# Decay factors of a state space layer: from PSUM one pair ahead to SBUF five pairs ahead

## The chip, the cores and the metric

The kernel runs on one core of a Trainium2 chip. The metric is the device time of one launch in microseconds (us). A core has TensorE (matrix products; PE in the profile, with PEld for its weight loads), VectorE (DVE), ScalarE (ACT), GpSimd (POOL) and SyncE (SP), which issues the DMAs here. Each engine works through its own queue in order, and they wait for one another by semaphores. SBUF is the on-chip working memory; PSUM, of eight banks, takes the results of TensorE.

## The reference

Two residual layers on an image batch `x` of 4 x 384 x 64 x 64, all in float32. Layer 0 is a state space layer: group norm, layer norm, a projection to 2 x 768 channels, a causal convolution of width 4, SiLU, a projection to the step `dt` and to B and C (16 states each), the recurrence, a gate, and a projection back. Layer 1 is attention in 7 x 7 windows. The change is in the recurrence of layer 0:

```python
dt = jax.nn.softplus(jnp.einsum('blr,dr->bld', dt, dt_w) + dt_b)
A = -jnp.exp(A_log)
def step(h, inp):
    dt_t, B_t, C_t, x_t = inp
    dA = jnp.exp(dt_t[:, :, None] * A[None])
    dBx = (dt_t * x_t)[:, :, None] * B_t[:, None, :]
    h = dA * h + dBx
    y_t = jnp.einsum('bdn,bn->bd', h, C_t)
    return (h, y_t)
...
y = jnp.moveaxis(ys, 0, 1) + xc * D
y = y * _silu(z)
out = jnp.einsum('bld,cd->blc', y, out_proj_w)
```

It runs over 4,096 time steps for each of 4 images, 768 channels and 16 states.

## The kernel before

Channels lie on the 128 partitions (six tiles `d` of 128), time along the free dimension. A step `I` takes 256 time steps of one image, so there are 4 x 16 = 64 steps. A *group* is four of the sixteen states (`g`) of one channel tile: 64 x 6 x 4 = 1,536 groups. In each group ScalarE computes the decay factors exp(A dt) for four states, VectorE runs four scans, GpSimd and VectorE multiply the states by C, and TensorE sums them. Beside this, a plan of 48 slots per step carries the preparation of the next steps (norms, projections, convolution, softplus) in between; one slot runs after each half group.

GpSimd makes the driving term `db` = dt x B of a group, two groups ahead:

```python
def driven(I, d, g, h):
    ...   # at g == 0: dtx = dt * xc, 128 x 256, on GpSimd
    db = w2.tile([P, NG, T], F32, tag="db", ..., bufs=3)
    nc.gpsimd.tensor_tensor(
        db, h["dtx"].unsqueeze(1).broadcast_to([P, NG, T]), h["bc"][g][0], ALU.mult
    )
    return db
```

The group itself. `ps_a` (two banks) holds the decay factors `da`, a pair of states to a bank; `ps_h` (one bank) holds the states `hp` of the first pair; those of the second pair, `hs`, lie in SBUF:

```python
def scan(I, d, g, h, db, y, ahead):
    dt = h["dt"][d // 2][:, d % 2, :]
    ct = h["bc"][g][1]
    hp = ps_h.tile([P, 2, T], F32, tag="hp", name="hp")
    hv = w2.tile([P, 2, T], F32, tag="hv", name="hv")
    hs = w2.tile([P, 2, T], F32, tag="hs", name="hs", bufs=4)
    for half, to in ((0, hp), (1, hs)):
        da = ps_a.tile([P, 2, T], F32, tag="da", name="da")
        n = g * NG + 2 * half
        for k in range(2):
            act(da[:, k, :], dt, AF.Exp, scale=nega[:, d, n + k : n + k + 1])
        for k in range(2):
            nc.vector.tensor_tensor_scan(
                to[:, k, :], da[:, k, :], db[:, 2 * half + k, :],
                state[:, d, n + k : n + k + 1] if I % NCHUNK else 0.0,
                ALU.mult, ALU.add,
            )
            if half == 1 and k == 0:
                nc.vector.tensor_copy(state[:, d, n - 2 : n], hp[:, :, T - 1])
                nc.vector.tensor_tensor(hv, hp, ct[:, 0:2, :], ALU.mult)
        ahead()          # one slot of the preparation

    def with_c():        # called during the next group
        nc.gpsimd.tensor_copy(state[:, d, n : n + 2], hs[:, :, T - 1])
        nc.gpsimd.tensor_tensor(hs, hs, ct[:, 2:4, :], ALU.mult)

    def summed(t):       # TensorE: transposes of hv or hs, summed in y
        ...
```

Two more places matter. Softplus ends with three VectorE instructions in one slot, each with a PSUM input (`pb`). And the group norm of each image, and of layer 1, works on three numbers per partition in SBUF:

```python
def added():             # softplus
    pb, dt = t["pb"], t["dt"]
    nc.vector.scalar_tensor_tensor(pb, pb, -1.0, t["e"], ALU.add, ALU.subtract)
    nc.vector.tensor_tensor(pb, t["r"], pb, ALU.subtract)
    nc.vector.tensor_tensor(dt, dt, pb, ALU.add)

def deviation():         # group norm; dev, mv and gm lie in SBUF
    nc.vector.tensor_copy(gm[:, :, 0], t["psmc"][:, 0:NJ])
    nc.vector.tensor_tensor(dev, mv[:, :, 0:1], gm[:, :, 0:1], ALU.subtract)
    nc.vector.tensor_tensor(dev, dev, dev, ALU.mult)
    nc.vector.tensor_tensor(dev, dev, mv[:, :, 1:2], ALU.add)
```

PSUM in layer 0: two banks for `da`, one for `hp`, two for `y`, three for the preparation. The weights of the attention layer, `w_qkv` and `w_pj`, are loaded at the start of the kernel and stay in SBUF throughout.

Of the kernel before, what the change touches and what calls it, by code (L numbers as in the profile page):

```python
# [8 lines left out]
F32 = mybir.dt.float32  # L9
AF = mybir.ActivationFunctionType  # L10
ALU = mybir.AluOpType
PSUM = bass.MemoryType.PSUM
DRAM = bass.MemoryType.DRAM

P = 128
# [10 lines left out]
NX = DTR + 2 * NS  # L26
T = 256
NCHUNK = L // T
TX = 512
NXT = L // TX  # L30
GROUPS = 32
# [17 lines left out]
def two_layers(  # L49
# [45 lines left out]
    def act(o, i, func, **kw):  # L95
        ins = nc.scalar.activation(o, i, func, **kw)  # L96
        return in_order(ins) if func in tabled else ins
# [54 lines left out]
    def load(shape, src, name):  # L152
        t = const.tile(shape, F32, name=name)
        nc.sync.dma_start(t, src)
        return t
# [41 lines left out]
    for j in range(NJ):  # L197
        nc.vector.tensor_scalar(w_in[:, j, :], w_in[:, j, :], lnw[:, j : j + 1], None, ALU.mult)


    w_qkv = const.tile([P, NJ, 3 * C], F32, name="w_qkv")
    nc.sync.dma_start(w_qkv, qkv_wT.rearrange("(k p) m -> p k m", p=P))
    w_pj = load([P, NJ, C], proj_wT.rearrange("(k p) m -> p k m", p=P), "w_pj")
    with tc.tile_pool(name="ps_vb", bufs=1, space=PSUM) as fps:
        pb0 = fps.tile([P, 512], F32, name="pvb")
        for m in range(NJ):
            for j in range(NJ):
                nc.tensor.matmul(
                    pb0[:, m : m + 1], w_pj[:, j, m * P : (m + 1) * P], qkb[:, 2 * NJ + j : 2 * NJ + j + 1],
                    start=(j == 0), stop=(j == NJ - 1),  # L210
                )
        nc.vector.tensor_tensor(pjb, pjb, pb0[:, :NJ], ALU.add)

    state = const.tile([P, ND, NS], F32, name="state")
    xb = const.tile([P, ND, KC - 1 + T], F32, name="xb")

# [66 lines left out]
    def layer0(x1s, mvs):  # L283

        with ExitStack() as es:
            es.enter_context(tc.manual_schedule(engines=in_step))
            ps_a = es.enter_context(tc.tile_pool(name="ps_a", bufs=2, space=PSUM))
            ps_h = es.enter_context(tc.tile_pool(name="ps_h", bufs=1, space=PSUM))
            ps_y = es.enter_context(tc.tile_pool(name="ps_y", bufs=2, space=PSUM))
            ps = es.enter_context(tc.tile_pool(name="ps0", bufs=3, space=PSUM))  # L290
            bc = es.enter_context(tc.tile_pool(name="bc", bufs=4))
            w1 = es.enter_context(tc.tile_pool(name="w1", bufs=1))
            w2 = es.enter_context(tc.tile_pool(name="w2", bufs=2))
# [116 lines left out]
            def prepared(I, h, at):  # L410
# [82 lines left out]
                def softplus(q, first):  # L493

                    t = {}

                    def project():
                        t["pb"] = bank()
                        for k in range(2):
                            nc.tensor.matmul(  # L500
                                t["pb"][:, k, :],
                                w_dt[:, (2 * q + k) * P : (2 * q + k + 1) * P],
                                h["xd"][:DTR, :], start=True, stop=True,
                            )

                    def parts():
                        t["e"] = w2.tile([P, 2, T], F32, tag="sp_e", name=f"spe_{b}_{i}_{q}")
                        t["r"] = w2.tile([P, 2, T], F32, tag="sp_r", name=f"spr_{b}_{i}_{q}")
                        for k in range(2):
                            bias = dtb[:, 2 * q + k : 2 * q + k + 1]  # L510
                            act(t["e"][:, k, :], t["pb"][:, k, :], AF.Abs, bias=bias)
                            act(t["r"][:, k, :], t["pb"][:, k, :], AF.Relu, bias=bias)

                    def exped():
                        act(t["e"], t["e"], AF.Exp, scale=-1.0)
                        act(t["pb"], t["e"], AF.Identity, bias=1.0)

                    def logged():
                        t["dt"] = w2.tile([P, 2, T], F32, tag="dt", name=f"dt_{b}_{i}_{q}", bufs=4)
                        act(t["dt"], t["pb"], AF.Ln)  # L520

                    def added():
                        pb, dt = t["pb"], t["dt"]
                        nc.vector.scalar_tensor_tensor(
                            pb, pb, -1.0, t["e"], ALU.add, ALU.subtract
                        )
                        nc.vector.tensor_tensor(pb, t["r"], pb, ALU.subtract)
                        nc.vector.tensor_tensor(dt, dt, pb, ALU.add)
                        h["dt"].append(dt)

                    at(first, project)
                    at(first + 2, parts)
                    at(first + 3, exped)
                    at(first + 4, logged)
                    at(first + 5, added)

                for q in range(ND // 2):
                    softplus(q, 33 + 3 * q)
# [13 lines left out]
                )  # L552
                return db

            def scan(I, d, g, h, db, y, ahead):



                dt = h["dt"][d // 2][:, d % 2, :]
                ct = h["bc"][g][1]  # L560
                hp = ps_h.tile([P, 2, T], F32, tag="hp", name="hp")
                hv = w2.tile([P, 2, T], F32, tag="hv", name="hv")
                hs = w2.tile([P, 2, T], F32, tag="hs", name="hs", bufs=4)
                for half, to in ((0, hp), (1, hs)):
                    da = ps_a.tile([P, 2, T], F32, tag="da", name="da")
                    n = g * NG + 2 * half
                    for k in range(2):
                        act(da[:, k, :], dt, AF.Exp, scale=nega[:, d, n + k : n + k + 1])
                    for k in range(2):
                        nc.vector.tensor_tensor_scan(  # L570
                            to[:, k, :], da[:, k, :], db[:, 2 * half + k, :],
                            state[:, d, n + k : n + k + 1] if I % NCHUNK else 0.0,
                            ALU.mult, ALU.add,
                        )
                        if half == 1 and k == 0:
                            nc.vector.tensor_copy(state[:, d, n - 2 : n], hp[:, :, T - 1])
                            nc.vector.tensor_tensor(hv, hp, ct[:, 0:2, :], ALU.mult)  # L577
                    ahead()

                def with_c():  # L580
                    nc.gpsimd.tensor_copy(state[:, d, n : n + 2], hs[:, :, T - 1])  # L581
                    nc.gpsimd.tensor_tensor(hs, hs, ct[:, 2:4, :], ALU.mult)  # L582

                def summed(t):

                    for k in range(2):
                        first = g == 0 and t is hv and k == 0
                        last = g == NS // NG - 1 and t is hs and k == 1
                        for half in range(2):
                            nc.tensor.matmul(  # L590
                                y[:, half, :], t[:, k, half * P : (half + 1) * P], ident,
                                is_transpose=True, start=(first and half == 0),
                                stop=(last and half == 1), skip_group_check=True,
                            )

                return with_c, lambda: summed(hv), lambda: summed(hs)

            def turned(I, d, h, yt):

# [107 lines left out]
            run(-2)  # L707
            run(-1)
            work = [(I, d, g) for I in range(STEPS) for d in range(ND) for g in range(NS // NG)]
            AHEAD = 2  # L710
            dbs = [driven(*w, steps[w[0]]) for w in work[:AHEAD]]
            before = []
            for n, (I, d, g) in enumerate(work):
                slots = iter(range(2 * (n % (SLOTS // 2)), SLOTS))

                def ahead():
                    s = next(slots)
                    run(I, s, s + 1)

                if g == 0:  # L720
                    steps[I]["yt"][d] = ps_y.tile([P, 2, P], F32, tag="y", name="y")
                if before:
                    before[0][0]()
                if n + AHEAD < len(work):
                    nxt = work[n + AHEAD]
                    dbs.append(driven(*nxt, steps[nxt[0]]))
                if before:
                    before[0][1]()
                if len(before) > 1:
                    before.pop()[2]()  # L730
                before.insert(
                    0, scan(I, d, g, steps[I], dbs.pop(0), steps[I]["yt"][d], ahead)
                )
            before[0][0]()
            before[0][1]()
            before[1][2]()
            before[0][2]()
            run(STEPS)

    def layer1(x1s, mvs):  # L740
        scale = HD**-0.5
        with ExitStack() as es:
# [6 lines left out]

            bias = wt.tile([P, NH, NK], F32, name="bias")  # L750
            nc.sync.dma_start(bias.rearrange("p h k -> p (h k)"), bm)
            gms, vds = [], []
            for b in range(NB):
                gms.append(small.tile([P, NJ, 2], F32, tag="gm1", name=f"gm_b{b}", bufs=NB))
# [329 lines left out]
```

## Time and profile before

| | |
|---|---|
| time, median of three | 9,433.48 us (9,431.37 to 9,436.09) |
| span of the profiled execution | 9,436.4 us |
| busy share over the span | TensorE 83%, VectorE 79%, GpSimd 65%, ScalarE 61% |
| layer 0, first scan to last product of GpSimd | 111.8 to 6,797.7 us |
| VectorE / GpSimd busy from 6,900 us on (2,536 us) | 1,458 / 84 us |

The page gives, for every group of like instructions, the line, the engine, output<-inputs by the tile's name, partitions x elements, the count, then the busy time in us, the mean length of one in ns, and the idle time of the engine ahead of it with what ended it. Records of one engine overlap a little at their ends, so the distance from start to start in the timeline is somewhat less than an instruction's recorded length. [...] A view of the busy time by stretch tells the two layers apart; the shares of the whole span mix them. L96 is the helper that issues every activation.

### The profile page before, as it was taken

What the parts mean: (1) busy time and instruction counts of PE and PEld (TensorE: products, weight loads), DVE (VectorE), ACT (ScalarE), POOL (GpSimd) and SP (SyncE); (2) the same over time, 40 slices, a digit from 0 to 9 for tenths busy, and PEclk for the clock granted to TensorE, in tenths of its full rate; (3) what the DMA queues carried; (4) which work ended last, traced back from release to release, by engine and by line L of the source; (5) the groups of instructions that cost most, each with busy time, mean ns of one, the idle gap of its engine ahead of it and who ended that gap; (6) DMA issues with size and microseconds to landing.
All of it is one profiled execution on the core that took longest, in us unless ns stands there. A gap on an engine that the chain in (4) does not pass through costs nothing.

```text
span 9436.4 us, 139560 instructions
## 1 busy us (share of the span) xinstructions
PE 7804.9 (83%) x46266; PEld 5722.8 (61%) x46266; DVE 7485.8 (79%) x15348; ACT 5773.9 (61%) x13694; POOL 6104.2 (65%) x5271
## 2 busy tenths in 40 slices
PE   7877887788777877787788777877789999999999
PEld 5666666666666666666666666666545555555555
DVE  6888988898889888988898888888755555555555
ACT  5666666666766676666666766676444444444444
POOL 5888988898989898988889989998700000000000
PEclk8887888788878888888788888887699999999999
DMA  3111111111111111111111111111122222222222
GB/s 107 51 49 61 54 51 43 58 54 51 49 59 55 47 45 61 54 51 49 59 50 47 43 57 48 47 43 59 51 72 77 67 80 76 74 77 78 75 76 62
DMA packets 301912, 557.92 MB, mean 59 GB/s; under 512 B 61916, under 2 KB 185580, under 8 KB 301060
## 3 DMA queue, kind: packets, MB, share of 16 engines
q1 hardware_dynamic: 301188, 549.00, 18.4%
q8 instruction: 365, 5.98, 0.3%
q14 instruction: 359, 2.94, 0.1%
HBM read 446.33 MB, written 84.73 MB: 56 GB/s over the span
## 4 chain that ended last, share of the span: by engine, by line
PE 36%; DVE 28%; ACT 16%; POOL 10%; issue 9%; DMA 0%; SPq 0%; DVEq 0%; ACTq 0%; POOLq 0%
DVE hp L570 9%; DVE hs L570 8%; POOL db L550 5%; DVE hv L577 5%; PE mm_ps L628 5%; ACT da L96 4%; POOL hs L582 4%; PE y L590 3%; ACT sg L96 3%; PE mm_ps L393 3%; PE lg_ps L887 3%; PE mm_ps L969 3%; PE mm_ps L792 3%; PE mm_ps L855 3%; PE pt_ps L912 2%
## 5 line engine op out<-in xcount | busy, mean ns | idle before, releaser
L96 ACT ACTIVATE da<-dt,nega 128x256 f32<-128x256 f32 x6144 | 2922.8, 477 | 1416.8 <-DVE hs L570 972.3
L550 POOL TENSOR_TENSOR db<-dtx,B 128x1024 f32<-128x1024 f32 x1536 | 3620.9, 2357 | 30.1
L570 DVE TENSOR_TENSOR_SCAN hs<-da,state,db 128x256 f32<-128x256 f32 x2880 | 2118.6, 736 | 347.8 <-ACT da L96 347.8
L570 DVE TENSOR_TENSOR_SCAN hp<-da,state,db 128x256 f32<-128x256 f32 x2880 | 2153.8, 748 | 303.0 <-POOL state L581 192.9
L582 POOL TENSOR_TENSOR hs<-hs,C 128x512 f32<-128x512 f32 x1536 | 1952.2, 1271 | 123.2 <-POOL state L581 0.8
L590 PE MATMUL y<-ident,hv 128*128 128x128 f32 x6144 | 1192.0, 327 | 960.5 <-DVE hv L577 953.8
L590 PEld LDWEIGHTS y<-ident,hv 128*128 128x128 f32 x6144 | 850.5, 165 | 1409.5 <-DVE hv L577 1292.1
L96 ACT ACTIVATE sg<-sg,mx 128x308 f32<-128x308 f32 x1536 | 830.0, 541 | 890.1 <-DVE mx L893 889.8
L946 POOL COPY rb<-rsum 128x384 f32<-128x384 f32 x128 | 65.4, 511 | 2017.0 <-DVE rsum L944 1901.5
L590 PE MATMUL y<-ident,hs 128*128 128x128 f32 x6144 | 1156.4, 321 | 137.1 <-POOL hs L582 135.6
L393 PE MATMUL mm_ps<-xn,w_in 128*128 128x256 f32 x4608 | 1163.9, 404 | 2.0 <-DVE xn L369 2.0
L577 DVE TENSOR_TENSOR hv<-hp,C 128x512 f32<-128x512 f32 x1536 | 1044.3, 680 | 0.0
L590 PEld LDWEIGHTS y<-ident,hs 128*128 128x128 f32 x6144 | 901.8, 169 | 184.0 <-POOL hs L582 180.4
L393 PEld LDWEIGHTS mm_ps<-xn,w_in 128*128 128x128 f32 x4608 | 925.3, 207 | 133.3 <-issue 3.4
L893 DVE CUSTOM_DVE_ANT_0 sg<-lg_ps,bias 128x308 f32<-128x308 f32 x1536 | 650.4, 474 | 261.1 <-PE lg_ps L887 258.4
L400 PE MATMUL mm_ps<-xb,dcv 128*128 128x256 f32 x3072 | 716.9, 379 | 0.0
L581 POOL COPY state<-hs 128x2 f32<-128x2 f32 x1536 | 289.7, 189 | 523.6 <-DVE hs L570 461.9
L400 PEld LDWEIGHTS mm_ps<-xb,dcv 128*128 128x128 f32 x3072 | 567.6, 190 | 72.5
L500 PE MATMUL mm_ps<-xd,w_dt 24*128 24x256 f32 x768 | 335.4, 577 | 289.9 <-DVE yg L617 287.0
L628 PE MATMUL mm_ps<-yg,w_out 128*128 128x256 f32 x2304 | 520.9, 380 | 0.0
L917 DVE COPY ta<-pt_ps 110x512 f32<-110x512 f32 x768 | 495.4, 680 | 24.1 <-PE pt_ps L912 21.4
L927 ACT COPY tb<-pt_ps 88x512 f32<-88x512 f32 x384 | 223.1, 581 | 392.2 <-PE pt_ps L923 392.2
(139 smaller groups left out, 10832.0 us busy)
## 6 DMA issues: line engine op xcount, KB each, us to landing
B<-bcrows SPq DMA_DIRECT2D x256, 512.0 KB
C<-bcrows SPq DMA_DIRECT2D x256, 512.0 KB
vw<-vd SPq DMA_DIRECT2D x1792, 33.0 KB
xr<-x SPq DMA_DIRECT2D x28, 1056.0 KB
vd<-v SPq DMA_DIRECT2D x280, 96.0 KB
xi<-in_x_dram SPq DMA_DIRECT2D x64, 384.0 KB
x<-xo SPq DMA_DIRECT2D x64, 384.0 KB
o<-x SPq DMA_DIRECT2D x96, 256.0 KB
```

The lines of the kernel that those rows point to most:

```text
L96: ins = nc.scalar.activation(o, i, func, **kw)
L393: nc.tensor.matmul(pb[:, k, :], w_in[:, j, m * P : (m + 1) * P], xn[:, j, :], start=(j == 0), stop=(j == NJ - 1),)
L400: nc.tensor.matmul(pb[:, k, :], dcv[:, d, c, :], xb[:, d, c : c + T], start=(c == 0), stop=(c == KC - 1),)
L500: nc.tensor.matmul(t["pb"][:, k, :], w_dt[:, (2 * q + k) * P : (2 * q + k + 1) * P], h["xd"][:DTR, :], start=True, stop=True,)
L550: nc.gpsimd.tensor_tensor(db, h["dtx"].unsqueeze(1).broadcast_to([P, NG, T]), h["bc"][g][0], ALU.mult)
L570: nc.vector.tensor_tensor_scan(to[:, k, :], da[:, k, :], db[:, 2 * half + k, :], state[:, d, n + k : n + k + 1] if I % NCHUNK else 0.0, AL ...
L577: nc.vector.tensor_tensor(hv, hp, ct[:, 0:2, :], ALU.mult)
L582: nc.gpsimd.tensor_tensor(hs, hs, ct[:, 2:4, :], ALU.mult)
L590: nc.tensor.matmul(y[:, half, :], t[:, k, half * P : (half + 1) * P], ident, is_transpose=True, start=(first and half == 0), stop=(last an ...
L628: nc.tensor.matmul(h["po", first][:, m - first, :], w_out[:, d, m * P : (m + 1) * P], h["yg"][d], start=(d == 0), stop=(d == ND - 1),)
L893: nc.vector.tensor_tensor_reduce(sg[:, hh, :], lg[:, :NK], bias[:, 4 * m + hh, :], -1.0, BIG, ALU.add, ALU.min, mx[:, hh : hh + 1],)
L917: nc.vector.tensor_copy(t[: KN[0], :, :].rearrange("p a q -> p (a q)"), pt[: KN[0], :])
```

## The change

It gives the decay factors a longer lead and moves the recurrence out of PSUM:

- `da` lies in SBUF, in seven buffers of a pair each, and ScalarE writes it five pairs ahead of the scans (before: two PSUM banks, just ahead of them).
- All four scans of a group write one SBUF tile `hs`. The product with C of the first pair is done in place by VectorE, of the second pair in place by GpSimd, both during the next group.
- The last column of all four states is kept by one VectorE instruction (a maximum of the column with itself). GpSimd no longer copies states.
- The three banks set free go to the preparation: six in place of three. The three VectorE instructions of softplus are spread over three slots.
- To make room in SBUF, the attention weights, and the small product with `w_pj`, move to the start of layer 1.

It is meant to keep the scans from waiting for ScalarE, which leaves its exponentials once in a step for SiLU and two table loads.

```diff
+LEAD = 5
-    w_qkv = const.tile([P, NJ, 3 * C], F32, name="w_qkv")
-    ...                                   # moved to layer1, with w_pj and pvb
-            ps_a = es.enter_context(tc.tile_pool(name="ps_a", bufs=2, space=PSUM))
-            ps_h = es.enter_context(tc.tile_pool(name="ps_h", bufs=1, space=PSUM))
-            ps = es.enter_context(tc.tile_pool(name="ps0", bufs=3, space=PSUM))
+            ps = es.enter_context(tc.tile_pool(name="ps0", bufs=6, space=PSUM))
...
-                    at(first + 5, added)
+                    at(first + 5, lost)
+                    at(first + 6, linear)
+                    at(first + 7, added)
...
-            def scan(I, d, g, h, db, y, ahead):
-            ...
+            def decay(I, d, g, half, h):
+                da = w2.tile([P, 2, T], F32, tag="da", name="da", bufs=LEAD + 2)
+                dt = h["dt"][d // 2][:, d % 2, :]
+                n = g * NG + 2 * half
+                for k in range(2):
+                    act(da[:, k, :], dt, AF.Exp, scale=nega[:, d, n + k : n + k + 1])
+                return da
+
+            def scans(I, d, g, half, h, da, db, hs, between):
+                for k in range(2):
+                    j = 2 * half + k
+                    n = g * NG + j
+                    nc.vector.tensor_tensor_scan(
+                        hs[:, j, :], da[:, k, :], db[:, j, :],
+                        state[:, d, n : n + 1] if I % NCHUNK else 0.0,
+                        ALU.mult, ALU.add,
+                    )
+                    if k == 0:
+                        between()
+
+            def product(d, g, h, hs, y):
+                ct = h["bc"][g][1]
+                def kept_and_first():
+                    end = hs[:, :, T - 1]
+                    nc.vector.tensor_tensor(
+                        state[:, d, g * NG : (g + 1) * NG], end, end, ALU.max
+                    )
+                    nc.vector.tensor_tensor(hs[:, 0:2, :], hs[:, 0:2, :], ct[:, 0:2, :], ALU.mult)
+                def second():
+                    nc.gpsimd.tensor_tensor(hs[:, 2:4, :], hs[:, 2:4, :], ct[:, 2:4, :], ALU.mult)
+                ...
+                return kept_and_first, second, summed
...                                        # in the loop over groups:
+                hs = w2.tile([P, NG, T], F32, tag="hs", name=f"hs_{I}_{d}_{g}", bufs=4)
+                db = dbs.pop(0)
+                for half in range(2):
+                    if 2 * n + half + LEAD < len(halves):
+                        nxt = halves[2 * n + half + LEAD]
+                        das.append(decay(*nxt, steps[nxt[0]]))
+                    between = after[0][0] if half == 0 and after else lambda: None
+                    scans(I, d, g, half, steps[I], das.pop(0), db, hs, between)
+                    if half == 0:
+                        if after:
+                            after[0][1]()
+                        if n + AHEAD < len(work):
+                            nxt = work[n + AHEAD]
+                            dbs.append(driven(*nxt, steps[nxt[0]]))
+                        if len(after) > 1:
+                            after.pop()[2]()
+                    s = 2 * n + half
+                    run(I, s % SLOTS, s % SLOTS + 1)
+                after.insert(0, product(d, g, steps[I], hs, steps[I]["yt"][d]))
```

## The prediction

> **What bounds the kernel now.** I read the page's busy shares first, then the busy time by stretch, which tells the two layers apart: the state space layer runs from about 112 us to 6,800 us, the attention layer after it. The change alters the first alone. The columns are the stretch, its length, and the busy time and instructions of each engine.

> ```profile
> core 0: us, PE busy (x) PEld busy (x) DVE busy (x) ACT busy (x) POOL busy (x), PEclk, DMA share, GB/s
> ...
> 3000.00:5000.00 2000.00, 1590.26 (x7822) 1291.99 (x7822) 1784.23 (x3208) 1359.28 (x2979) 1791.68 (x1507) 0.82 0.16 52
> ```

> VectorE and GpSimd are both busy for 89% of these 2,000 us; TensorE for 80%, ScalarE for 68%. So two engines run side by side near their limits. The groups on the page say with what (count, busy us, mean ns of one, idle before):

> ```profile
> L550 POOL TENSOR_TENSOR db<-dtx,B 128x1024 f32<-128x1024 f32 x1536 | 3620.9, 2357 | 30.1
> L570 DVE TENSOR_TENSOR_SCAN hs<-da,state,db 128x256 f32<-128x256 f32 x2880 | 2118.6, 736 | 347.8 <-ACT da L96 347.8
> L570 DVE TENSOR_TENSOR_SCAN hp<-da,state,db 128x256 f32<-128x256 f32 x2880 | 2153.8, 748 | 303.0 <-POOL state L581 192.9
> L582 POOL TENSOR_TENSOR hs<-hs,C 128x512 f32<-128x512 f32 x1536 | 1952.2, 1271 | 123.2 <-POOL state L581 0.8
> ...
> L577 DVE TENSOR_TENSOR hv<-hp,C 128x512 f32<-128x512 f32 x1536 | 1044.3, 680 | 0.0
> ```

> [...]From the first scan (111.8 us) to the end of the last product on GpSimd (6,797.7 us) a group takes 6,686 / 1,536 = 4.35 us. The chain of waits for the stretch 3,000 to 5,000 us (458 groups) shows where VectorE idles:

> ```profile
> DVE hs L570 <- ACT da L96: 112.7, 74, 3.1
> DVE hp L570 <- POOL state L581: 61.3, 19, 3.6
> DVE hp L570 <- ACT da L96: 11.9, 18, 1.3
> ```

> Together 186 us, or 0.41 us a group. These are the waits that the change goes after: a longer lead of the exponentials, and no copy of the state on GpSimd.

> The line that decides is elsewhere. VectorE's tensor_tensor on `dev_a` has three elements a row and both inputs in SBUF. Here are VectorE and, below, GpSimd at the same time (start us, us, engine, line):

> ```profile
> 4799.84 0.47 DVE L264 TENSOR_TENSOR dev_a<-mv,gm_a 128x3 f32<-128x3 f32 x1
> 4800.34 0.16 DVE L265 TENSOR_TENSOR dev_a<-dev_a 128x3 f32<-128x3 f32 x1
> 4800.53 1.26 DVE L266 TENSOR_TENSOR dev_a<-dev_a,mv 128x3 f32<-128x3 f32 x1
> ```
> ```profile
> 4797.93 2.36 POOL L550 TENSOR_TENSOR db<-dtx,B 128x1024 f32<-128x1024 f32 x1
> 4800.22 0.20 POOL L581 COPY state<-hs 128x2 f32<-128x2 f32 x1
> 4800.50 1.28 POOL L582 TENSOR_TENSOR hs<-hs,C 128x512 f32<-128x512 f32 x1
> ```

> L264 ends at 4800.31, as GpSimd's L550 does (4800.29); L266 ends at 4801.79, as L582 does (4801.78). The same instruction in the attention layer, where GpSimd is idle:

> ```profile
> L266 DVE TENSOR_TENSOR dev_b<-dev_b,mv x4: 161/161/161, 6814.2 to 6832.5; 128x3 f32<-128x3 f32 x4
> ```

> 0.16 us against 1.26 us: a VectorE instruction with two SBUF inputs stands still until GpSimd's tensor_tensor is through. The reader should now look at the loop: scan (`da` in PSUM, `db` in SBUF), `hv` (`hp` in PSUM, C in SBUF), softplus, gate, residual, each has one input in PSUM. `hv` took 680 ns in every group (673 to 684), whatever GpSimd did.

> [...] a scan of 256 columns into SBUF starts 0.64 us after the one before it, a tensor_tensor of 512 columns 0.60 us. [...] here `da` (PSUM) takes 477 ns and `xn`, SBUF to SBUF with one pointer more, 585 ns. No trace here has `da` in SBUF.

> **The change, part by part**, per group:
> 1. *Exponentials in SBUF, five pairs ahead.* Four activations remain, at most 585 instead of 477 ns, so up to 0.4 us more on ScalarE, which has 4.35 x 0.32 = 1.4 us free. What it removes is up to 0.25 to 0.27 us of VectorE's idle time (112.7 + 11.9 us over 458 groups). What it adds: every scan now has both inputs, `da` and `db`, in SBUF.
> 2. *Scans to SBUF.* The two of a group that wrote PSUM start 0.72 us apart (two `hp` scans take 1.44 us), those that write SBUF 0.64: saves 2 x 0.08 = 0.16 us.
> 3. *The state copy* moves from GpSimd (0.19 us, with its start gap 0.27) to one VectorE tensor_tensor, and `hv` becomes a product in place, `hs` by C. Both have two SBUF inputs. Lengths 0.1 (my choice between the copy's 0.05 and the 0.19 of a dependent small tensor_tensor) and 0.60 us.
> 4. *Six banks for the preparation, softplus in three slots, the attention weights loaded later.* Same instructions. The weights are 128 x 4,608 x 4 bytes = 2.36 MB; at the 164 GB/s that the turn between the layers shows this is 14 us, once. I count 0 to 15 us.

> [...] VectorE: 4 scans x 0.64 + 0.60 + 0.1 = 3.26 us. GpSimd: L264 ended 0.02 us after L550 though it needs 0.16 alone, so GpSimd lets go about 0.14 us ahead of its record's end: 2.36 - 0.14 = 2.22 for `db`, 1.27 - 0.14 = 1.13 for the product, (0.73 - 0.14) / 4 = 0.15 for `dtx`; 3.50 us. VectorE's other instructions (softplus, gate, norm, statistics: the remaining rows of the groups by form in that stretch add up to some 265 us, 0.58 us a group) read PSUM or one SBUF input and can run beside GpSimd, but the queue is in order; I count half, 0.29. Sum 3.26 + 3.50 + 0.29 = 7.05, less 0.15 that I choose for the start of VectorE's instructions, done while they wait: **6.9 us a group**. Against 4.35 that is 2.55 x 1,536 = 3,917 us more: 9,433 + 3,917 = **13,350 us**. The 0.41 us of idle that the longer lead takes away doesn't help, since it stands beside a longer serial path.

> **Rivals.**
> - *It works as meant* (no contention). VectorE would need 4 x 0.64 + 0.60 + 0.1 + 0.58 = 3.84 us, GpSimd 2.29 + 1.23 + 0.2 = 3.72 us from start to start. With little idle left, some 3.95 us a group: 9,433 - 0.4 x 1,536 = about 8,800 us. Against it: the two waits on `dev_a`, and that the `hv` product has just the form of L266.
> - *Only the tensor_tensors contend, the scan doesn't.* No scan in this trace has two SBUF inputs, so it isn't excluded. GpSimd's 3.72 plus 0.60 plus 0.1 is 4.4 us at the least, and some VectorE time lost behind it: 4.4 to 4.9 us, 9,500 to 10,300 us.
> - *ScalarE or TensorE becomes the bound.* TensorE is busy 1,590 / 458 = 3.47 us a group, ScalarE 2.97 + 0.4. Both stay below 4.35, so neither alone makes it slower.

> **Range and chances.** A group time of 6.1 to 7.5 us covers what I chose: [...] how the two engines alternate. That is 9,433 + 1.75 x 1,536 = 12,100 to 9,433 + 3.15 x 1,536 = 14,300 us (rounded). The whole of it rests on the scan contending; I give the first rival 4 in 100 and the second about 10, of which some 4 end within 2%. So faster by over 2%: 0.04; within 2%: 0.04; slower by over 2%: 0.92.

> **What the profile after will show.** If right: scan records with a mean well over 1 us, a share of them near 0.65 and others about one GpSimd instruction longer; VectorE and GpSimd both busy nearly all of a layer that is 10 to 11 ms long[...]; records of `db` longer than 2.36 us where GpSimd waits in turn; no waits of scans for `da`; a TensorE clock no lower than now. The attention layer stays at 2.5 ms. Wrong: scans of 0.64 to 0.75 us each while `db` runs[...].

## The result and the profile after

The changed kernel takes **13,101 us** (median of four, 13,099.76 to 13,103.59) against 9,435 us before on the same chip: a ratio of 1.389, interval 1.386 to 1.391. The prediction was 13,350 us, in a range of 12,100 to 14,300.

The busy time by stretch, as it was shown for before (VectorE 1,784 us, GpSimd 1,792 us of 2,000 there):

```profile
3000.00:5000.00 2000.00, 1270.41 (x5056) 911.07 (x5056) 1989.63 (x2079) 854.23 (x1915) 1387.20 (x679) 0.72 0.11 35
```

VectorE is busy for 99.5% of it and runs a third fewer instructions (2,079 for 3,208). The groups on the page say which became longer:

```profile
L559 DVE TENSOR_TENSOR_SCAN hs<-da,state,db 128x256 f32<-128x256 f32 x5760 | 8091.8, 1448 | 0.0
L97 ACT ACTIVATE da<-dt,nega 128x256 f32<-128x256 f32 x6144 | 2784.5, 500 | 5882.7 <-DVE hs L559 5881.9
...
L580 POOL TENSOR_TENSOR hs<-hs,C 128x512 f32<-128x512 f32 x1536 | 2623.6, 1708 | 3120.1 <-DVE state L574 2589.3
L540 POOL TENSOR_TENSOR db<-dtx,B 128x1024 f32<-128x1024 f32 x1536 | 4173.3, 2717 | 30.1
```

A scan takes 1,448 ns on the mean, not 736 or 748. Its idle time is 0.0: no scan waits for a semaphore, and the exponentials wait 5,882 us for the scans. What the change went after is gone. In its place the scan itself is longer: it stands still while it counts as busy. GpSimd's instructions are longer too, 2,717 for 2,357 ns and 1,708 for 1,271: it waits in its turn.

One group in the timelines of VectorE and GpSimd (start us, us):

```profile
5022.45 0.13 DVE L574 TENSOR_TENSOR state<-hs 128x4 f32<-128x4 f32 x1
5022.61 0.69 DVE L577 TENSOR_TENSOR hs<-hs,C 128x512 f32<-128x512 f32 x1
5023.22 5.74 DVE L559 TENSOR_TENSOR_SCAN hs<-da,state,db 128x256 f32<-128x256 f32 x4
```
```profile
5022.72 1.71 POOL L580 TENSOR_TENSOR hs<-hs,C 128x512 f32<-128x512 f32 x1 [2.03 <-DVE state L574]
5024.39 2.73 POOL L540 TENSOR_TENSOR db<-dtx,B 128x1024 f32<-128x1024 f32 x1
```

They take turns. GpSimd's product (issued 5022.72) waits for VectorE's product (`hs` by C, to 5023.30) and then runs to 5024.43. The first scan, issued at 5023.22, waits for it. `db`, issued at 5024.39, waits for that scan, then holds the next one until 5027.12. Scans of 1.75 and 2.77 us are followed by two of 0.72, while GpSimd has nothing to do and waits for the next group's state. The least and the greatest length of all scans are near those of this group, and most scans have one of its three lengths: of 5,760, 2,645 take 0.7 to 0.8 us, 1,440 take 1.7 to 1.8 and 897 take 2.7 to 2.8.

```profile
L559 DVE TENSOR_TENSOR_SCAN hs<-da,state,db x5760: 716/1150/2789, 268.0 to 10451.9; 128x256 f32<-128x256 f32 x199
```

From the first scan to the last product the layer takes 10,342 us, 6.73 us a group for 4.35 before. From that product to the end it takes 2,646 us for 2,639: the attention layer costs 7 us more, with its weights loaded there.

### The profile page after: what moved, and what is told of

The parts are those of the page before. It is cut to its first block, busy times and chain, and to the rows that moved or that the text cites. A ratio compares the mean times of both kernels' runs of the same rounds, so it can differ in the third digit from the quotient of the medians.

```text
span 13100.7 us, 137829 instructions
## 1 busy us (share of the span) xinstructions
PE 9036.2 (69%) x46266; PEld 6092.5 (47%) x46266; DVE 11805.3 (90%) x15348; ACT 5673.7 (43%) x13694; POOL 7285.8 (56%) x3735
## 4 chain that ended last, share of the span: by engine, by line
DVE 72%; PE 16%; issue 8%; ACT 4%; SPq 0%; DMA 0%; POOL 0%; DVEq 0%; ACTq 0%; POOLq 0%
DVE hs L559 61%; ACT sg L97 2%; DVE hs L577 2%; PE lg_ps L903 2%; PE mm_ps L808 2%; PE mm_ps L985 2%; PE mm_ps L871 2%; PE pt_ps L928 2%; PE pv_ps L951 2%; PE mm_ps L841 2%; PE pt_ps L939 1%; DVE yg L615 1%; DVE state L574 1%; DVE mm_ps L508 1%; DVE mm_ps L513 1%
## 5 line engine op out<-in xcount | busy, mean ns | idle before, releaser
L559 DVE TENSOR_TENSOR_SCAN hs<-da,state,db 128x256 f32<-128x256 f32 x5760 | 8091.8, 1448 | 0.0
L588 PE MATMUL y<-ident,hs 128*128 128x128 f32 x12288 | 2675.5, 361 | 3352.2 <-DVE hs L577 3079.5
L580 POOL TENSOR_TENSOR hs<-hs,C 128x512 f32<-128x512 f32 x1536 | 2623.6, 1708 | 3120.1 <-DVE state L574 2589.3
L540 POOL TENSOR_TENSOR db<-dtx,B 128x1024 f32<-128x1024 f32 x1536 | 4173.3, 2717 | 30.1
L588 PEld LDWEIGHTS y<-ident,hs 128*128 128x128 f32 x12288 | 1784.7, 180 | 4420.4 <-DVE hs L577 2580.9
L577 DVE TENSOR_TENSOR hs<-hs,C 128x512 f32<-128x512 f32 x1536 | 1064.0, 693 | 53.3
L559 DVE TENSOR_TENSOR_SCAN hs<-da,db 128x256 f32<-128x256 f32 x384 | 528.0, 1419 | 0.0
L626 PEld LDWEIGHTS mm_ps<-yg,w_out 128*128 128x128 f32 x2304 | 483.0, 215 | 73.6
L535 POOL TENSOR_TENSOR dtx<-dt,xc 128x256 f32<-128x256 f32 x384 | 425.9, 1109 | 103.3 <-DVE dt L516 103.3
L928 PE MATMUL pt_ps<-ident,sg 128*110 128x128 f32 x3072 | 416.7, 277 | 0.0
```

Source lines behind the costliest of these rows:

```text
L540: nc.gpsimd.tensor_tensor(db, h["dtx"].unsqueeze(1).broadcast_to([P, NG, T]), h["bc"][g][0], ALU.mult)
L559: nc.vector.tensor_tensor_scan(hs[:, j, :], da[:, k, :], db[:, j, :], state[:, d, n : n + 1] if I % NCHUNK else 0.0, ALU.mult, ALU.add,)
L577: nc.vector.tensor_tensor(hs[:, 0:2, :], hs[:, 0:2, :], ct[:, 0:2, :], ALU.mult)
L580: nc.gpsimd.tensor_tensor(hs[:, 2:4, :], hs[:, 2:4, :], ct[:, 2:4, :], ALU.mult)
L588: nc.tensor.matmul(y[:, half, :], hs[:, k, half * P : (half + 1) * P], ident, is_transpose=True, start=(first and half == 0), stop=(last a ...
L626: nc.tensor.matmul(h["po", first][:, m - first, :], w_out[:, d, m * P : (m + 1) * P], h["yg"][d], start=(d == 0), stop=(d == ND - 1),)
```

## Experiments

The theory, from the two instructions on `dev_a` (0.47 and 1.26 us in place of 0.16): a VectorE instruction with two SBUF inputs and a GpSimd instruction that reads SBUF run one after the other, and so the scans with both inputs in SBUF add their time to that of GpSimd's work. Rivals: the new order, the scans into SBUF or the in-place products cost the time; the scan is slow from SBUF by itself; only the tensor_tensors contend. Where no interval is given, a time is that of a single execution.

**Decay factors back in PSUM**, the rest as changed.

```diff
-LEAD = 5
+LEAD = 1
-                da = w2.tile([P, 2, T], F32, tag="da", name="da", bufs=LEAD + 2)
+                da = ps_a.tile([P, 2, T], F32, tag="da", name="da")   # 3 banks; ps0: 3
```

> The changed kernel with one thing undone: the decay factors lie in PSUM again (three banks, one pair ahead, three banks left for the preparation). Scans then have one SBUF input; only the state copy and the product of the first pair keep two. Theory [...]: scans 0.65 us from start to start, a group of 4.4 to 4.9 us, 9,500 to 10,300 us in all. Rival (the new order of the instructions, the scans into SBUF or the in-place products cost the time): stays above 12,500 us, with scans of 1.1 to 1.4 us on the mean.

Measured: 9,778 us. The groups on its page:

```profile
L560 DVE TENSOR_TENSOR_SCAN hs<-da,state,db 128x256 f32<-128x256 f32 x5760 | 3953.3, 732 | 127.8 <-ACT da L97 125.9
...
L575 DVE TENSOR_TENSOR state<-hs 128x4 f32<-128x4 f32 x1536 | 1184.2, 771 | 0.0
...
L578 DVE TENSOR_TENSOR hs<-hs,C 128x512 f32<-128x512 f32 x1536 | 1063.0, 692 | 52.7
```

Scans are back at 732 ns: new order, in-place products and output in SBUF stay (the preparation has three banks again), and 3,320 of the 3,670 us are gone. It is still 342 us slower than the kernel before (9,436 on its chip). The page shows what stands still now: the state's maximum, with two SBUF inputs, takes 771 ns for four columns where 133 suffice in the changed kernel, 0.64 x 1,536 = 980 us behind GpSimd.

**Only the decay factors into SBUF**, in the kernel before. With their two buffers that pool of SBUF tiles takes 95 KB a partition, and the attention weights leave it 91.4, so these are loaded at the start of layer 1, as in the changed kernel.

```diff
-                    da = ps_a.tile([P, 2, T], F32, tag="da", name="da")
+                    da = w2.tile([P, 2, T], F32, tag="da", name="da")     # 2 buffers, as in PSUM
...                                         # w_qkv, w_pj and pvb moved to layer 1
```

> The kernel before with one thing done: the decay factors in SBUF, two buffers as in PSUM, all else as before (first pair of states in PSUM, its product with a PSUM input; the attention weights are loaded at the start of layer 1 as in the changed kernel, to make room). Theory [...]: the scans alone contend with GpSimd; 2.7 us of scans and about 3.6 us of GpSimd's reading stand one behind the other, a part of the rest beside them: a group of 6.2 to 6.8 us, 12,300 to 13,200 us. Rival (the scan doesn't contend, the tensor_tensors with two SBUF inputs do): within 3% of 9,434 us.

Measured: 13,021 us, 98% of the whole loss. Three rows of its page:

```profile
L556 DVE TENSOR_TENSOR_SCAN hs<-da,state,db 128x256 f32<-128x256 f32 x2880 | 4308.3, 1496 | 72.1 <-ACT da L96 72.1
...
L556 DVE TENSOR_TENSOR_SCAN hp<-da,state,db 128x256 f32<-128x256 f32 x2880 | 3750.6, 1302 | 157.8 <-ACT da L96 5.1
...
L563 DVE TENSOR_TENSOR hv<-hp,C 128x512 f32<-128x512 f32 x1536 | 1036.8, 675 | 0.0
```

Both kinds of scan are longer. The product `hv` still has its PSUM input and takes 675 ns (680 before): it doesn't wait. GpSimd's copy of the state, which has one input, takes 503 ns for 189: it waits in its turn. So the scan itself contends, and "only the tensor_tensors" is out. The later weights account for some 6 us of the loss (2,645 us from the last product to the end, for 2,639).

**GpSimd writes but doesn't read.** The driving term, its product with C and dtx are left out; the tiles are filled with a constant.

```diff
-                nc.gpsimd.tensor_tensor(db, ..., h["bc"][g][0], ALU.mult)
+                nc.gpsimd.memset(db, 0.001)
+                nc.gpsimd.memset(db, 0.001)      # the same for hs[:, 2:4, :]; once for dtx
```

> The changed kernel with GpSimd's driving term, its products with C and dtx left out; in their place GpSimd fills the same tiles with a constant, twice each, so that it is busy for about as long (some 3.3 us a group) but reads nothing. The output is another one. Theory [...]: scans 0.65 us, no waiting, a group of 3.9 to 4.1 us, 8,700 to 9,100 us in all. Rival A (a scan with both inputs in SBUF is slow by itself): stays near 13,100 us. Rival B (GpSimd's writes, or its being busy at all, hold VectorE): 12,000 us or more.

Measured: 8,689 us. The same stretch, then the scans' group in 2,000 us of the layer:

```profile
3000.00:5000.00 2000.00, 1657.61 (x8863) 1376.93 (x8862) 1971.76 (x3621) 1463.63 (x3359) 1537.92 (x2224) 0.88 0.17 57
```
```profile
L555 DVE TENSOR_TENSOR_SCAN hs<-da,state,db 128x256 f32<-128x256 f32 x1986 | 1362.5, 734 | 0.0
```

GpSimd is busy for 77% of the time and VectorE doesn't notice. A scan with both inputs in SBUF takes 734 ns. It isn't slow by itself, and neither GpSimd's writes nor its being busy hold it, nor ScalarE's writes of `da`, which go on as changed. What is missing is GpSimd's reads. A memset is another instruction than a tensor_tensor, but the copy above, which reads as well, was held too (503 ns for 189). A group takes 3.86 us: about what the change would have brought had GpSimd's reads not held the scans.

**Only the driving term left out.**

```diff
-                nc.gpsimd.tensor_tensor(db, ..., h["bc"][g][0], ALU.mult)
+                nc.gpsimd.memset(db, 0.001)      # twice; product with C and dtx as changed
```

> The changed kernel with only the driving term left out (GpSimd fills it with a constant, twice); its product with C of the second pair and dtx stay and read SBUF. Theory[...]: the 2.1 to 2.2 us of the driving term leave the serial path, a group of 4.5 to 5.1 us, 9,700 to 10,600 us. Rival (VectorE loses a fixed time at each meeting, whatever the length of GpSimd's instruction): about half of the loss stays, 11,000 us or more.

Measured: 10,334 us, 4.93 us a group:

```profile
L558 DVE TENSOR_TENSOR_SCAN hs<-da,state,db 128x256 f32<-128x256 f32 x5760 | 5508.1, 1000 | 0.0
```

Of the 6.73 - 3.86 = 2.87 us that GpSimd's reads cost, the driving term takes 1.80 and the rest 1.07. In the kernel before, the driving term took 2.36 us of GpSimd and the rest, the product and a quarter of a dtx, 1.27 + 0.18 = 1.45. So each costs about three quarters of its length (0.76 and 0.74): the loss follows how long GpSimd reads. By the number of meetings (1 and 1.25 a group) the rest would have cost the more.

**One pair ahead in place of five.**

```diff
-LEAD = 5
+LEAD = 1
```

> The changed kernel with the decay factors written one pair ahead in place of five (three buffers in place of seven). Theory [...]: ScalarE isn't on the path, a pair of scans takes 2.8 us on the mean and ScalarE leaves for some 7 us once in a step, so a wait of at most 3 to 4 us a step comes up, part of it beside GpSimd's reading: 13,050 to 13,350 us. Rival (the long lead itself costs or gains much): a change of over 3% from 13,101 us.

Measured: 13,100 us, as with five. The scans are so slow that a lead of one pair suffices.

**Shorter instructions on GpSimd.**

```diff
-                nc.gpsimd.tensor_tensor(db, dtx broadcast over NG, ..., ALU.mult)
+                for k in range(NG):
+                    nc.gpsimd.tensor_tensor(db[:, k, :], h["dtx"], h["bc"][g][0][:, k, :], ALU.mult)
```

> The changed kernel with GpSimd's driving term cut into four instructions of 128 x 256, one per state. Theory [...]: the longest scan falls from 2.8 to about 1.3 us[...]: 13,000 to 13,900 us. Rival (long instructions are the trouble, short ones slip in between): under 12,500 us.

Measured: 12,592 us, between the two ranges, nearer to the rival's. The longest scan falls from 2.79 to 1.77 us, the mean to 1,255 ns, but the state's maximum now waits as well (498 ns), as GpSimd still has pieces to do when it comes. That scans get in between the pieces is what the theory has; that none of the loss goes is wrong by 14% of it (3,157 for 3,666 us). No run shows where these 14% went.

**The state without a second SBUF input**, in the first experiment's kernel.

```diff
-                    nc.vector.tensor_tensor(state[...], end, end, ALU.max)
+                    nc.vector.tensor_reduce(state[...], hs[:, :, T - 1 : T], mybir.AxisListType.X, ALU.max)
```

> The first experiment's kernel (decay factors in PSUM, one pair ahead, all scans into SBUF) with the state kept by a tensor_reduce over one element, which has one SBUF input, in place of the maximum of the column with itself, which has two. Theory: the 0.64 us that the maximum stood behind GpSimd goes; what stays is GpSimd standing 0.44 us behind the product of the first pair. A group of 4.1 to 4.35 us, bound by GpSimd's 4.16 us: 9,150 to 9,450 us against 9,778. Rival (the wait only moves to the product, which now meets the driving term): 9,600 to 9,800 us.

Measured: 9,580 us, 1.016 of before (1.014 to 1.018): my expectation missed, the rival's was nearly met. Two rows of its groups in 2,000 us:

```profile
L579 DVE TENSOR_TENSOR hs<-hs,C 128x512 f32<-128x512 f32 x450 | 532.6, 1184 | 15.5
...
L575 DVE TENSOR_REDUCE state<-hs 128x4 f32<-128x4 f32 x450 | 57.4, 128 | 0.0
```

The reduction takes 128 ns and doesn't wait (158 at the most). Three quarters of the wait moved to the next instruction with two SBUF inputs: the maximum had taken 0.64 us longer than that, and the product now takes 1,184 ns in place of 692, 0.49 us longer.

**The same reduction in the kernel before**, in place of GpSimd's copy of the state, run after the first scan of the next group.

```diff
-                    nc.gpsimd.tensor_copy(state[:, d, n : n + 2], hs[:, :, T - 1])
+                    nc.vector.tensor_reduce(state[:, d, n : n + 2], hs[:, :, T - 1 : T], mybir.AxisListType.X, ALU.max)
```

> The kernel before with GpSimd's copy of the state moved to VectorE as a tensor_reduce with one SBUF input, run after the first scan of the next group. GpSimd loses 0.27 us a group from start to start, VectorE gets 0.07 to 0.15 more. Theory: VectorE with its waits for ScalarE bounds the group, GpSimd only at the burst of SiLU; the two cancel within 1.5%: 9,350 to 9,550 us. Rival (GpSimd's 4.0 us a group is the bound, and its copy stands on the path): 9,000 to 9,250 us.

Measured: 9,421 us, 0.999 (0.997 to 1.000). Among VectorE's waits in the stretch 3,000 to 5,000 us:

```profile
DVE hp L570 <- issue: 61.6, 19, 4.0
```

GpSimd's copy wasn't on the path; the 61 us that the waits of before, and my prediction with them, put down to it stay, now without a releaser named. They are the burst of SiLU on ScalarE: up to the end of such a wait of 3.55 us (3100.79 to 3104.34) ScalarE runs six activations for SiLU, a table load of 1.28 us and then the two exponentials that the scan needs.

That left the change's aim, the lead, to be had with `da` in PSUM. **The queue's order alone**: in the kernel before, the exponentials of the next pair are issued ahead of this pair's slot of preparation, with the banks as they were.

```diff
+            def decayed():                  # decay(): the four lines that scan() had
+                while len(das) < LEAD + 1 and (v := next(halves, None)):     # LEAD = 1
+                    das.append(decay(*v, steps[v[0]]))
+                return das.pop(0)
...
-                    da = ps_a.tile([P, 2, T], F32, tag="da", name="da")      # and the two act()
+                    da = decayed()
```

> The kernel before with the exponentials of the next pair placed ahead of the scans of this one in ScalarE's queue, the banks as they were (two for the decay factors). Theory: with two banks the pair can be written only when the pair before the last has been scanned, so the queue's order changes little, and the preparation in ScalarE's queue now waits behind it: 9,350 to 9,650 us. Rival (the order is what lacked): 9,150 to 9,300 us.

Measured: 9,196 us, 0.975 (0.973 to 0.976). I was wrong: with only two banks the order was what lacked. Slot work in ScalarE's queue had stood ahead of exponentials that were needed sooner. VectorE's waits for them are 100 us of 2,000, for 186 before (125, and the 61 of the burst):

```profile
DVE hs L576 <- ACT da L97: 60.1, 44, 3.2
DVE hp L576 <- ACT da L97: 39.7, 61, 1.3
```

**Three banks in PSUM**, with that order; the bank is taken from `y`, whose tile is summed to its end before the next one starts.

```diff
-            ps_a = es.enter_context(tc.tile_pool(name="ps_a", bufs=2, space=PSUM))
+            ps_a = es.enter_context(tc.tile_pool(name="ps_a", bufs=3, space=PSUM))
-            ps_y = es.enter_context(tc.tile_pool(name="ps_y", bufs=2, space=PSUM))
+            ps_y = es.enter_context(tc.tile_pool(name="ps_y", bufs=1, space=PSUM))
-                    turn(I, d, h, slot_of(I), (d + 1) * (SLOTS // ND) + 4)
+                    turn(I, d, h, slot_of(I), (d + 1) * (SLOTS // ND) + 2)
...                                         # sums of hs(n-2) before those of hv(n-1)
```

> The kernel before with the decay factors in three PSUM banks and one pair ahead in ScalarE's queue; the bank is taken from the sums y (one in place of two; they are read two slots earlier, and TensorE sums a finished tile before it starts the next). All two-input instructions of VectorE keep one input in PSUM. Theory: the lead is to be had in PSUM[...]: VectorE's waits for ScalarE fall from 0.27 to about 0.1 us a group and the burst gets shorter: 9,050 to 9,300 us. Rival (TensorE now waits for the one bank of y, and the preparation behind it holds ScalarE): 9,450 us or more.

Measured: 9,171 us, 0.972 (0.970 to 0.973), little beyond the order alone. With three banks a longer lead is possible:

```diff
-LEAD = 1
+LEAD = 2
```

> The kernel with three PSUM banks for the decay factors and one for y (before 9,171 us), with the exponentials two pairs ahead in ScalarE's queue in place of one. Theory: what VectorE still waits for ScalarE (87 us in 2,000 us, 0.18 a group) comes from the burst of SiLU; one more pair covers about 2 us of it each step, 64 steps: 9,000 to 9,130 us. Rival (ScalarE's own wait for TensorE at the one bank of y, 205 us in 2,000, is what is left): 9,140 to 9,250 us.

Measured: 9,089 us, 0.963 (0.962 to 0.965). And, with that, y read a slot later:

```diff
-                    turn(I, d, h, slot_of(I), (d + 1) * (SLOTS // ND) + 2)
+                    turn(I, d, h, slot_of(I), (d + 1) * (SLOTS // ND) + 3)
```

> The same with y read three slots after its last group in place of two. Theory: ScalarE no longer stands at the read of y, TensorE waits for the bank instead, with nothing behind it in a hurry: 8,980 to 9,130 us, at or below the one beside it. Rival (TensorE's wait holds the preparation): above the one beside it by 20 us or more.

Measured: **9,075 us**, 0.962 (0.960 to 0.964) of before; it beats both kernels. VectorE's longest waits in the stretch 3,000 to 5,000 us:

```profile
DVE xn L370 <- PE mm_ps L364: 27.5, 20, 2.5
DVE hp L576 <- ACT da L97: 17.7, 19, 1.3
DVE hs L576 <- ACT da L97: 14.7, 21, 0.9
DVE hp L576 <- POOL db L551: 14.4, 44, 0.6
```

The waits for `da` are 32 us of 2,000, for 125 before, and the burst's stall of up to 3.6 us is gone. A group takes 4.12 us.

## Why the prediction was right

**The line that decided was read rightly.** Two tensor_tensors of three elements, held for 0.47 and 1.26 us until GpSimd was through, told that `da` in SBUF would put the scans behind GpSimd. The scan with two SBUF inputs, of which the trace before had no example, does the same (1,448 ns on the mean for 736); moving `da` alone costs 98% of the loss, and taking GpSimd's reads away takes all of it back.

**The sum was right to 0.17 us a group because two terms missed in opposite directions.** Predicted: 3.26 + 3.50 + 0.29 - 0.15 = 6.9; measured: 6.73. The run in which GpSimd reads nothing has 3.86 us a group for VectorE alone. Its scans, state and product are 4 x 0.65 + 0.17 + 0.61 = 3.38 (predicted 3.26; the state starts 0.17 us ahead of the product, not 0.1). So its other instructions take 0.48, nearly all of what they need, where I counted half, 0.29. GpSimd's reads then cost 2.87 us, where I counted 3.50 less 0.15. I had taken 0.29 us off VectorE's other instructions, as lying beside GpSimd, and 0.15 off the whole; it was to be taken off GpSimd's reads instead, and more of it: 3.50 - 2.87 = 0.63 us. That GpSimd's reading adds to VectorE's time was right, though with 2.87 of its 3.81 us a group only; that the total came within 2% is in part luck.

**Point by point.**
- Scans near 0.65 to 0.75 us, and others longer by about one GpSimd instruction: right (2,645 of 5,760 below 0.8 us, 1,440 near 1.75, 897 near 2.77).
- Longer `db` records where GpSimd waits in turn: right, 2,717 ns for 2,357. The waiting goes in both directions, which the trace before didn't show.
- No scan waits for `da`: right, and the lead is worth nothing there (13,100 us with one pair). An exponential takes 500 ns into SBUF, where I allowed up to 585.
- "Both busy nearly all of the layer": wrong for GpSimd, 69%. Its product needs the state, which VectorE keeps only in the next group; after `db` it idles some 2 us in most.
- "A TensorE clock no lower than now": wrong, 0.72 for 0.82 in the same stretch.
- The rivals: "works as meant" was put at 8,800 us; it takes 8,689 once GpSimd reads nothing. "Only the tensor_tensors contend" was put at 9,500 to 10,300 us; the kernel built so, with `da` in PSUM, takes 9,778. Both sums held, but neither described the change.

## What to carry to other kernels

Where VectorE and GpSimd run side by side, count the SBUF inputs of each VectorE instruction. Here `da` in PSUM was worth 3,320 to 3,590 us and a better lead 360, and the maximum of four columns with two SBUF inputs stood for up to 2.0 us (median 0.92) in the first experiment. Taking away one such instruction may move most of the wait to the next one. Where the scans had two SBUF inputs, 2.87 us of GpSimd's 3.81 us a group were added to VectorE's time. To lengthen a lead, look first at the order in the producer's queue and at which PSUM bank can be shared; here that brought 3.8%.
